# The router's chain of the first pair of batches, emitted in front of the last product of the combined weights

## The chip, the cores and the metric

The kernel runs on one core of one Trainium2 chip. The metric is the device time of one execution in microseconds (us), and of several runs the median. The core has five engines that run side by side, each with its own queue, executed in order: TensorE (PE; its weight loads are listed as PEld), VectorE (DVE), ScalarE (ACT), GpSimd (POOL) and SyncE (SP), which here only starts transfers.

## What is computed

Two layers are added to x (32 batches of 128 tokens with 1024 channels, float32). The first is a mixture of 64 experts. The second maps each token through a dense matrix W plus a low-rank adapter of its batch, and on the result computes a base projection plus a routed low-rank term:

```python
def _L1_cond_ref(x, W, A, Bm, scalings, adapter_idx):
    H = jnp.einsum('btd,od->bto', x, W)
    xa = jnp.einsum('btd,brd->btr', x, A[adapter_idx])
    delta = jnp.einsum('btr,bor->bto', xa, Bm[adapter_idx])
    return H + delta * scalings[adapter_idx][:, None, None]

def _L1_ffn_ref(x, base_w, base_b, router_w, router_b, lora_A, lora_B):
    result = jnp.einsum('bsd,od->bso', x, base_w) + base_b
    logits = jnp.einsum('bsd,ed->bse', x, router_w) + router_b
    probs = jax.nn.softmax(logits.astype(jnp.float32), axis=-1)
    top_vals, top_idx = jax.lax.top_k(probs, 2)
    top_vals = top_vals / jnp.sum(top_vals, axis=-1, keepdims=True)
    gate = jnp.zeros((n, e), x.dtype).at[jnp.arange(n)[:, None], flat_idx].set(flat_val)
    mid = jnp.einsum('nd,edr->ner', xf, lora_A) * gate[:, :, None]
    lora_out = jnp.einsum('ner,erd->nd', mid, lora_B)
    return result + SCALING * lora_out.reshape(b, s, d_out)

x = x + _L0_ffn_ref(_L0_cond_ref(x, ...), ...)
x = x + _L1_ffn_ref(_L1_cond_ref(x, ...), ...)
```

## The kernel before

The first some 2045 us are the mixture of experts. The change lies in the passage from there to the second layer, which takes the rest of the time.

The second layer is done with combined weights: the products of W (and, as a ninth row block, of the adapters' matrices Bm) with the base projection, the low-rank matrices A and the router. They were computed earlier for two of three blocks of columns. The third block is computed in the passage, in `pair_of_rows` (line 1212), four pairs of row blocks with seven products each, and by `multiplied` (line 1259) for the ninth row block. The latter is called the last product here: eight matmuls 128x384 into the bank pcw. Line 1260 copies it with ScalarE into row 9 (`HC + 1`) of `BM`, the big matrix of the second layer, whose rows 0 to 7 belong to the channels, row 8 (`HC`) to the routed low-rank term and row 9 to the adapter.

The tokens are taken in pairs of batches, `q` from 0 to 15. For each pair `X` holds 256 tokens, transposed, in ten chunks: 0 to 7 are channels, chunk 8 is the routed term (mid) and chunk 9 the adapter's (xm). Pair 0 is prepared in the passage, pair q + 1 during iteration q of the loop. The preparation of a pair is this:

- `turned_x1`: two transposes on VectorE from `xq`, the rows loaded from memory, into chunks 0 to 7.
- `inner`: products px on TensorE, which give the low-rank values, the router's logits and the adapter's values; copies into pxs, and xm on VectorE.
- `turned_in` with chunk 9: two transposes on TensorE into a bank pt, a copy on ScalarE into `X`.
- `corrected`: two matmuls pg on TensorE, the adapter's share of the logits.
- `routed` (line 1108): the router's chain. VectorE adds pg to pxs, forms the logits lg and their negated maximum nmaxc; ScalarE computes two exponentials exc; VectorE finds the two largest (topc, idxc), the weights and at last mid. Of its operations only the two exponentials are on ScalarE, none is on TensorE.
- `turned_in` with chunk 8: the transposes pt of mid on TensorE, the copy into `X` on ScalarE.
- `token_sums2`: sums of parts of `X` on VectorE (names ss, and one in place in `X`).

`map_sums` (line 1006) forms on VectorE the four sums of parts of `BM` (names ts1, ts2, ts4, and one in place in `BM`). The loop then has seven products of five matmuls each for every pair, `product2(k)` (bank name pr_c), of which `product2(1)` and `product2(6)` come first: number 1 reads even rows of `BM` and even chunks of `X`, chunk 8 as its last; number 6 reads ts2 and ss2. The px of the next pair follow.

All engines are addressed through `InOrder`, a helper that keeps each engine's instructions in the order in which they are emitted in the source, so that the order of the source's lines is the order in each engine's queue. As this helper issues every operation, the profile shows one line, L219, for nearly all; the names of the tiles tell them apart. The table that ScalarE needs for the exponentials is loaded by an instruction of its own, which the build puts right in front of the first exponential that needs it.

Of the kernel before, what the change touches and what calls it, by code (L numbers as in the profile page):

```python
# [51 lines left out]
def kernel(  # L52
# [147 lines left out]
    def multiplied(n, d, hw, left, pool, tag, pe):  # L200
        w = BLOCKS[n][1] - BLOCKS[n][0]
        pcw = pool.tile([P, 512], F32, name=f"pcw_{n}_{d}", tag=tag)[:, 0:w]
        for j in range(HC):
            if j == HC // 2:
                yield
            pe.matmul(pcw, left[d][:, j, :], hw[:, j, :], start=(j == 0), stop=(j == HC - 1))
        yield pcw
# [859 lines left out]
    def inner(q, X):  # L1067
        px = pc_x.tile([P, 2, NA], F32, name=f"px_{q}", tag="px")
        for t in range(2):
            for j in range(HC):  # L1070
                pe.matmul(
                    px[:, t, :],
                    X[:, j, t * P : (t + 1) * P],
                    pxw[t][:, j, :],
                    start=(j == 0),
                    stop=(j == HC - 1),
                )
        pxs = c2.tile([P, 2, NX], F32, name=f"pxs_{q}", tag="pxs")
        act.copy(pxs, px[:, :, 0:NX])

        xm = c2.tile([P, 2, E2, R], F32, name=f"xm_{q}", tag="xm")
        dve.tensor_tensor(
            xm,
            px[:, :, NX:NA].unsqueeze(2).to_broadcast([P, 2, E2, R]),
            smask[:, 2 * q : 2 * q + 2, :].unsqueeze(3).to_broadcast([P, 2, E2, R]),
            ALU.mult,
        )
        return pxs, xm

    def turned_in(q, X, chunk, m):  # L1090
        pt = pc_t.tile([P, 2, P], F32, name=f"pt_{q}_{chunk}", tag="pt")
        for t in range(2):
            pe.transpose(pt[:, t, :], m[:, t].rearrange("p e r -> p (e r)"), ident)
        act.copy(X[:, chunk, :], pt.rearrange("p t c -> p (t c)"))

    def corrected(q, X, pxs):
        pg = pc_x.tile([P, 2, NX], F32, name=f"pg_{q}", tag="pg")
        for t in range(2):
            pe.matmul(
                pg[:, t, :],  # L1100
                X[:, HC + 1, t * P : (t + 1) * P],
                G_sb[:, 0:NX],
                start=True,
                stop=True,
            )
        return pg

    def routed(q, pxs, pg):
        dve.tensor_tensor(pxs, pxs, pg, ALU.add)

        lg = c2.tile([P, 2, E2], F32, name=f"lg_{q}", tag="lg")
        dve.tensor_tensor(
            lg, pxs[:, :, E2 * R : NX], rb_bc.unsqueeze(1).to_broadcast([P, 2, E2]), ALU.add
        )
        nmax = c2.tile([P, 2], F32, name=f"nmaxc_{q}", tag="nmaxc")
        dve.tensor_reduce(nmax, lg, AX.X, ALU.max, negate=True)
        ex = c2.tile([P, 2, E2], F32, name=f"exc_{q}", tag="exc")
        top = c2.tile([P, 2, 8], F32, name=f"topc_{q}", tag="topc")
        idx = c2.tile([P, 2, 8], U32, name=f"idxc_{q}", tag="idxc")
        for t in range(2):  # L1120
            act.activation(ex[:, t, :], lg[:, t, :], AF.Exp, bias=nmax[:, t : t + 1])
        for t in range(2):
            dve.max(top[:, t, :], ex[:, t, :])
            dve.max_index(idx[:, t, :], top[:, t, :], ex[:, t, :])
        idxf = c2.tile([P, 2, 2], F32, name=f"idxfc_{q}", tag="idxfc")
        dve.tensor_copy(idxf, idx[:, :, 0:2])
        tsum = c2.tile([P, 2], F32, name=f"tsumc_{q}", tag="tsumc")
        dve.tensor_reduce(tsum, top[:, :, 0:2], AX.X, ALU.add)
        rtop = c2.tile([P, 2], F32, name=f"rtopc_{q}", tag="rtopc")
        dve.reciprocal(rtop, tsum)  # L1130
        gv = c2.tile([P, 2, 2], F32, name=f"gv_{q}", tag="gv")
        dve.scalar_tensor_tensor(
            gv,
            top[:, :, 0:2],
            LORA_SCALING,
            rtop.unsqueeze(2).to_broadcast([P, 2, 2]),
            ALU.mult,
            ALU.mult,
        )
        pick = c2.tile([P, 2, 2, E2], F32, name=f"pick_{q}", tag="pick")  # L1140
        for t in range(2):
            dve.tensor_tensor(
                pick[:, t],
                iota_t[:, 0:E2].unsqueeze(1).to_broadcast([P, 2, E2]),
                idxf[:, t, :].unsqueeze(2).to_broadcast([P, 2, E2]),
                ALU.is_equal,
            )
        dve.tensor_tensor(
            pick, pick, gv.unsqueeze(3).to_broadcast([P, 2, 2, E2]), ALU.mult
        )  # L1150
        gate = c2.tile([P, 2, E2], F32, name=f"gate_{q}", tag="gate")
        dve.tensor_tensor(gate, pick[:, :, 0, :], pick[:, :, 1, :], ALU.add)
        mid = c2.tile([P, 2, E2, R], F32, name=f"mid_{q}", tag="mid")
        dve.tensor_tensor(
            mid,
            pxs[:, :, 0 : E2 * R].rearrange("p t (e r) -> p t e r", e=E2),
            gate.unsqueeze(3).to_broadcast([P, 2, E2, R]),
            ALU.mult,
        )
        return mid  # L1160
# [66 lines left out]
    for c in range(HC // 2):  # L1227
        pair = pair_of_rows(c, rows)
        next(pair)
        if c == 3:  # L1230
# [3 lines left out]
            pxs, xm = inner(0, X)  # L1234
# [21 lines left out]
        for _ in pair:  # L1256
            pass
    pg = corrected(0, X, pxs)
    _, pcw = multiplied(2, HC, hw, lefts, pc_p, "pp", pe)
    act.copy(BM[:, HC + 1, :, first:512], pcw.rearrange("p (n c) -> p n c", n=2))  # L1260
    mid = routed(0, pxs, pg)
    turned_in(0, X, HC, mid)
    sums = map_sums(first, 512)
    next(sums)
# [15 lines left out]
    for q in range(NQP):  # L1280
# [31 lines left out]
        if more:  # L1312
            own_columns(ab)
            pxs, xm = inner(q + 1, X)
# [10 lines left out]
        if more:  # L1325
            mid = routed(q + 1, pxs, corrected(q + 1, X, pxs))
# [94 lines left out]
```

## Time and profile before

| | us |
|---|---|
| median of 3 runs | 2678.86 (2677.95 to 2679.11) |
| profiled execution | 2666.59 |
| its span, first to last instruction | 2664.7 |
| TensorE busy | 2642.8 (99%) |
| VectorE busy | 1866.7 (70%) |
| ScalarE busy | 548.5 (21%) |
| mean granted TensorE clock | 0.999 of full |

A matmul in float32 stands in the trace as two records, so the eight matmuls of pcw are shown as x16. Times of instructions are counted from the start of the span. The durations of neighbouring instructions on one engine can overlap a little, since they are pipelined; starts are the safer measure. "ACT_TABLE_LOAD" occurs three times in the whole execution, each of 1.28 us: at the start, when the experts' stage begins (254.40 us), and in the passage.

### The profile page before, as it was taken

The numbers are of one execution on the slowest core, as the hardware profiler recorded it, in microseconds if no ns is written. First come the engines' busy times: TensorE is split into PE (matmuls) and PEld (weight loads), VectorE is DVE, ScalarE is ACT, GpSimd is POOL, SyncE is SP. The second block draws the span as 40 slices with busy tenths as digits, with TensorE's granted clock in tenths as the row PEclk, the third lists the DMA queues.
The fourth block names the chain that finished last, engine by engine and source line by source line (L and its number), as shares of the span: only waits on it lengthen the run. The fifth ranks groups of instructions, "written<-read, shape, count | busy, mean of one in ns | idle before, by whom it ended". The sixth has DMA issues, their size and how long they took to land.

```text
span 2664.7 us, 25525 instructions
## 1 busy us (share of the span) xinstructions
PE 2642.8 (99%) x8942; PEld 1507.4 (57%) x8942; DVE 1866.7 (70%) x3051; ACT 548.5 (21%) x1174; POOL 1051.1 (39%) x854
## 2 busy tenths in 40 slices
PE   8999999999999999999999999999999999999999
PEld 8985555555555555555555555555556655554554
DVE  4456888888888888888888888878776644444442
ACT  2331222222222222222222222222222100000000
POOL 3115546546455464555555555464441100000000
PEclk9999999999999999999999999999999999999999
DMA  9869788788787887887887887878877422222110
GB/s 349 322 242 365 228 253 263 236 251 266 234 258 252 246 269 229 262 259 236 263 249 247 252 255 243 258 251 240 252 230 217 89 67 67 68 67 67 56 38 37
DMA packets 126656, 568.45 MB, mean 213 GB/s; under 512 B 22960, under 2 KB 48816, under 8 KB 100672
## 3 DMA queue, kind: packets, MB, share of 16 engines
q1 hardware_dynamic: 65952, 383.16, 41.0%
q0 software_dynamic: 52384, 161.60, 24.3%
q10 hardware_dynamic: 8192, 22.06, 2.2%
q8 instruction: 72, 1.18, 0.2%
q14 instruction: 56, 0.46, 0.1%
HBM read 459.68 MB, written 123.83 MB: 219 GB/s over the span
## 4 chain that ended last, share of the span: by engine, by line
PE 95%; DMA 3%; POOL 1%; DVE 0%; issue 0%; ACT 0%; ACTq 0%; SPq 0%
PE px L219 27%; PE pr_c L219 18%; PE pv L219 12%; PE py L219 6%; PE pth L219 2%; PE ph L219 2%; PE plog L219 1%; PE pcw L219 1%; DMA hw<-in_head_w 1%; PE pcx L219 1%; PE pmx L219 1%; DMA xin<-hbuf,slot_row 1%; DMA hbuf<-hq 1%; POOL xin L382 1%; PE prk L219 1%
## 5 line engine op out<-in xcount | busy, mean ns | idle before, releaser
L382 POOL DMA_INDIRECT xin<-hbuf,slot_row x512 | 609.5, 1190 | 169.4 <-issue 148.4
L960 POOL DMA_INDIRECT ybuf<-o,slot_tok x128 | 208.5, 1629 | 682.9 <-DVE o L219 234.3
L219 PE MATMUL pr_c<-BM,X 128*128 128x512 f32 x480 | 214.9, 595 | 0.0
L219 POOL DMA_INDIRECT ab<-in_AT,adapter_rows x32 | 37.2, 1163 | 424.4 <-ACT pxw L219 419.0
L306 POOL DMA_INDIRECT rkg<-ranks,row x128 | 157.1, 1227 | 85.1 <-DVE past L219 46.4
L219 PE MATMUL px<-wg,xT 128*128 128x384 f32 x512 | 186.1, 486 | 0.6 <-ACT G_sb L219 0.6
L219 PE MATMUL pv<-t,s 128*128 128x384 f32 x512 | 175.7, 486 | 0.0
L219 PE MATMUL px<-wu,xT 128*128 128x384 f32 x512 | 175.6, 486 | 0.0
L219 PE MATMUL pv<-wu,s 128*128 128x384 f32 x512 | 175.6, 486 | 0.0
L219 PE MATMUL px<-t,xT 128*128 128x384 f32 x512 | 175.6, 486 | 0.0
L219 PE MATMUL py<-wg,xT 128*128 128x384 f32 x512 | 175.6, 486 | 0.0
L219 PE MATMUL px<-t,s 128*128 128x384 f32 x512 | 175.6, 486 | 0.0
L219 DVE TENSOR_TENSOR t<-wu,wg 128x1536 f32<-128x1536 f32 x64 | 113.1, 1768 | 74.4 <-PE pv L219 74.4
L219 DVE STREAM_TRANSPOSE xT<-xin 128x1024 f32<-128x1024 f32 x128 | 151.7, 1220 | 13.2 <-DMA xin<-hbuf,slot_row 10.8
L219 ACT COPY u<-px 128x384 f32<-128x384 f32 x128 | 61.3, 479 | 434.0 <-PE px L219 434.0
L219 PEld LDWEIGHTS pr_c<-BM,X 128*128 128x128 f32 x480 | 89.4, 191 | 100.8 <-issue 100.8
L219 PEld LDWEIGHTS pv<-t,s 128*128 128x128 f32 x512 | 97.2, 190 | 81.0 <-issue 25.8
L219 PE MATMUL pr_c<-ts,ss 128*128 128x512 f32 x320 | 142.4, 592 | 0.0
L219 PEld LDWEIGHTS px<-t,s 128*128 128x128 f32 x512 | 97.3, 190 | 67.8
L219 PEld LDWEIGHTS py<-wg,xT 128*128 128x128 f32 x512 | 97.3, 190 | 67.8
L219 PEld LDWEIGHTS px<-wu,xT 128*128 128x128 f32 x512 | 97.3, 190 | 67.8
L219 PEld LDWEIGHTS pv<-wu,s 128*128 128x128 f32 x512 | 97.3, 190 | 67.8
(1576 smaller groups left out, 4549.6 us busy)
## 6 DMA issues: line engine op xcount, KB each, us to landing
wd<-in_wd SPq DMA_DIRECT2D x64, 1536.0 KB, 8.2
wg<-in_wg SPq DMA_DIRECT2D x63, 1536.0 KB, 8.2
wu<-in_wu SPq DMA_DIRECT2D x63, 1536.0 KB, 10.2
hbuf<-hq ACTq DMA_DIRECT2D x32, 512.0 KB, 8.5
ybuf<-in_x SPq DMA_DIRECT2D x32, 512.0 KB, 8.5
xq<-ybuf SPq DMA_DIRECT2D x64, 256.0 KB, 5.0
out_y<-out_c SPq DMA_DIRECT2D x31, 512.0 KB, 2.7
x<-in_x_q SPq DMA_DIRECT2D x28, 512.0 KB, 7.7
```

The source lines that it names most:

```text
L219: return lambda *args, **kw: kept(op(*args, **kw))
L306: nc.gpsimd.indirect_dma_start(out=some["rk"][:, s, :, :].rearrange("p i t -> p (i t)"), out_offset=None, in_=ranks.rearrange("e b i t -> ...
L382: nc.gpsimd.indirect_dma_start(out=xin[:, q, :], out_offset=None, in_=quarters, in_offset=bass.IndirectOffsetOnAxis(ap=slot_row[:, s : s + ...
L960: nc.gpsimd.indirect_dma_start(out=ybuf, out_offset=bass.IndirectOffsetOnAxis(ap=slot_tok[:, s : s + 1], axis=0), in_=o[j], in_offset=None ...
```

## The change

One line moves. The router's chain of pair 0 is emitted after `corrected` and ahead of the last product and its copy, instead of after them:

```diff
     pg = corrected(0, X, pxs)
+    mid = routed(0, pxs, pg)
     _, pcw = multiplied(2, HC, hw, lefts, pc_p, "pp", pe)
     act.copy(BM[:, HC + 1, :, first:512], pcw.rearrange("p (n c) -> p n c", n=2))
-    mid = routed(0, pxs, pg)
     turned_in(0, X, HC, mid)
     sums = map_sums(first, 512)
     next(sums)
```

The loop's own calls of `routed` are not touched.

## The prediction

> **What bounds the kernel now.** I read the shares of busy time first, then the chain that ended last, then the waits of TensorE, and only then the stretch of the change.
>
> ```profile
> PE 2642.8 (99%) x8942; PEld 1507.4 (57%) x8942; DVE 1866.7 (70%) x3051; ACT 548.5 (21%) x1174; POOL 1051.1 (39%) x854
> PE 95%; DMA 3%; POOL 1%; DVE 0%; issue 0%; ACT 0%; ACTq 0%; SPq 0%
> ```
>
> TensorE is busy for 99% of the span and is 95% of the chain, so a change pays only where TensorE stands still or runs below its full clock. The view of waits, for TensorE alone, has few entries:
>
> ```profile
> PE ph L219 <- DMA w<-in_cond_w,cond_rows: 9.0, 1, 9.0
> PE pt L219 <- DVE mid L219: 4.7, 1, 4.7
> PE pth L219 <- DVE h L219: 1.8, 1, 1.8
> ```
>
> The second is the place of the change: once, for 4.7 us, the transposes of mid wait for VectorE. The same view from 2115 us to the end is empty, so whatever is won here reaches the end whole. The timelines of TensorE, ScalarE and VectorE show how the wait comes about (start, duration, engine, operation; in brackets the idle time before it):
>
> ```profile
> 2093.09 5.32 PE L219 MATMUL pcw<-hw,WB_b 128*128 128x384 f32 x16
> 2103.13 0.69 PE L219 MATMUL pt<-ident,mid 128*128 128x128 f32 x2 [4.72 <-DVE mid L219]
> 2103.61 5.68 PE L219 MATMUL pr_c<-BM,X 128*128 128x512 f32 x10
> 2109.13 4.45 PE L219 MATMUL pr_c<-ts,ss 128*128 128x512 f32 x10
> 2113.42 4.30 PE L219 MATMUL px<-pxw,X 128*128 128x152 f32 x32
> ```
>
> ```profile
> 2092.88 0.32 ACT L219 COPY ts<-pmx 128x192 f32<-128x192 f32 x1 [2.28 <-PE pmx L219]
> 2098.45 0.48 ACT L219 COPY BM<-pcw 128x384 f32<-128x384 f32 x1 [5.25 <-PE pcw L219]
> 2098.94 1.28 ACT L219 ACT_TABLE_LOAD   x1
> 2100.24 0.49 ACT L219 ACTIVATE exc<-lg,nmaxc 128x8 f32<-128x8 f32 x2
> 2103.86 0.37 ACT L219 COPY X<-pt 128x256 f32<-128x256 f32 x1 [3.13 <-PE pt L219]
> ```
>
> ```profile
> 2094.44 0.17 DVE L219 TENSOR_REDUCE nmaxc<-lg 128x2 f32<-128x16 f32 x1
> 2100.57 0.17 DVE L219 MAX8 topc<-exc 128x8 f32<-128x8 f32 x1 [5.96 <-ACT exc L219]
> ...
> 2104.26 0.83 DVE L219 TENSOR_TENSOR ss<-X 128x640 f32<-128x640 f32 x1
> ...
> 2111.15 2.36 DVE L219 STREAM_TRANSPOSE X<-xq 128x1024 f32<-128x1024 f32 x2
> ```
>
> The router's maximum is ready at 2094.61, but its exponentials stand on ScalarE behind the copy of the last product, which TensorE ends at 2098.42. The table load and the exponentials come after that copy, and VectorE's remaining router steps after those. The wait costs more than its length, as the stretches of 3.41 us behind it show (the number after the POOL column is the granted TensorE clock):
>
> ```profile
> 2099.25:2102.66 3.41, 0.00 (x0) 0.00 (x0) 1.81 (x15) 1.47 (x3) 0.00 (x0) 1.00 0.18 32
> 2102.66:2106.07 3.41, 2.94 (x5) 1.50 (x6) 3.26 (x5) 0.77 (x3) 1.01 (x1) 0.50 0.00 0
> 2106.07:2109.50 3.43, 3.43 (x9) 1.52 (x8) 3.43 (x5) 0.00 (x0) 1.62 (x1) 1.00 0.12 38
> ```
>
> An idle stretch is followed by one of equal length at clock 0.50, in which the first product of the loop runs.
>
> **The change, part by part.** It adds and removes no instruction and no transfer. TensorE's order stays (pg, pcw, pt, pr_c), as routed puts nothing on TensorE; so does VectorE's, as the last product and its copy put nothing there; SP and POOL are not touched. On ScalarE the two exponentials, with the table load that stands ahead of them, move in front of the copy of pcw into BM.
>
> Step 1, the router's chain. The copy that precedes them on ScalarE ends at 2092.88 + 0.32 = 2093.20. The load then takes 1.28, to 2094.48; its cover is the last product, on TensorE until 2098.42. The maximum is there at 2094.61. Where the loop runs the same chain with the table in place, VectorE's MAX8 starts 0.37 us after the maximum; so here it starts at 2094.98. From MAX8 to the end of mid takes 2100.57 to 2103.08 = 2.51 us. Mid is ready at 2097.49.
>
> Step 2, TensorE. The records of pcw start 5.17/16 = 0.32 us apart, the last at 2097.92, so the transposes may start at 2098.25. Mid is there 0.76 us before: the wait of 4.72 us goes, and with it the slow clock. At full clock a pair of transposes takes 0.22 us start to start (those of xm at 2089.80 to 2090.02) and a product of five matmuls 4.29 (2109.13 to 2113.42), against 0.48 and 5.52 here. So on TensorE alone: transposes 2098.25, first product 2098.47, second 2102.76, px 2107.05, which is 6.37 us ahead of 2113.42 (4.88 of start, 0.26 and 1.23 of clock).
>
> The rule of the Trainium skill that speaks against this is in "ScalarE: Activation LUTs", section "What ACT_TABLE_LOAD costs": a switch of the table set is a load of about 1283 ns and a drain of about 1380 ns more. The load agrees (1.28 us); of a drain the row shows nothing, since the load starts 0.01 us after the copy and the exponential 0.02 us after the load. By the rule mid would come at 2097.49 + 1.38 = 2098.87, the transposes 0.62 us after TensorE is free, and the gain of the sum below would be 5.4 us instead of 5.9. I go by the row.
>
> Step 3, the copy that is now behind. It starts at 2098.45 as before if the exponentials are done, which they are from about 2095.2. The copy of the transposes into X (chunk 8) follows it. It needs the transposes (start + 0.42, as at 2089.80 to 2090.22: 2098.67) and ScalarE, whose copies overlap their neighbour by 0.1 us (the next one starts at 2104.13, before 2103.86 + 0.37): 2098.45 + 0.48 - 0.1 = about 2098.82.
>
> Step 4, what is late next. VectorE's sum ss started 0.40 us after that copy's start (2103.86 to 2104.26), so it starts at 2099.22, 5.04 us earlier. Behind it VectorE is unbroken to the transposes of the second pair of batches: they shift by 5.04 too. The first ended at 2111.15 + 1.23 = 2112.38, hence 2107.34, and px waits for it: TensorE would be there at 2107.05. The handoff is 0.05 (mid at 2103.08 to pt at 2103.13), and the weight load of px, hidden before, is, I estimate, exposed for 0.1 to 0.2 us (it takes 0.19). So px starts at about 2107.5 and the gain is 5.9 us. Bounds: 6.4, TensorE alone, and 5.7, if the copies on ScalarE don't overlap at all.
>
> Other work in the stretch hides: the sum ts1 needs nothing of pcw (it reads even rows of BM; the copy writes row 9) and runs while VectorE waits for X; ts2 ends at 2107.02 - 5.04 = 2101.98, 0.8 us before the second product can start. The bias and the rows of the second pair land by about 2100 (the DMA share is 0.86 from 2092 to 2100 and 0.10 in the next 1 us), and VectorE wants them only from 2105.5 on. The copies into pxw follow the copy into X on ScalarE, and POOL's two gathers follow these; both shift with it and are wanted an iteration later.
>
> The sum: 5.9 us of the profiled execution's 2666.59 (span 2664.7 and 1.9 around it). The median of the timed runs, 2678.86, lies 12.3 us higher; nothing in the stretch scales with that, so I take the gain as absolute: 2678.86 - 5.9 = 2673.0.
>
> **Rivals.**
> - *The timed executions of before did not pay the slow clock.* For: the idle 4.72 us is only 1.3 us longer than one of the 3.41 us stretches, so where the stretches lie may decide, and the three runs lie 1.16 us apart. Against: the profiled one did pay it. With a full clock, px of before would be ready at 2103.13 + 0.22 + 8.58 = 2111.93 and wait for VectorE's 2112.38; only the shift of VectorE is won, 5.0 us: 2673.9. That the clock is judged in free-running windows of about 3.4 us, so that the phase varies by run, is what the Trainium skill says in "TensorE: Matmul & The Clock Gate", section "What's actually happening"; the trace agrees in one place, with a drop 4.24 us after TensorE stopped.
> - *The router's chain ends after pcw.* A load of twice its row, 2.57 us, puts mid at 2098.77, leaves 0.52 us of idle in front of the transposes and puts the copy into X at 2099.19 and ss at 2099.59: a shift of 4.67, gain 5.5, 2673.4. Against: no row shows more than 1.28.
> - *VectorE or a transfer holds px longer,* by 1 to 3 us: gain 3 to 5, about 2674.9. For: VectorE is without a break there and 70% busy overall. Against: all that it reads has landed by 2100.
> - *Slower: ScalarE's head is blocked.* The table load waits, in the built instruction stream, for a count of a DMA queue. If that count were reached only with the rows of the second pair, at about 2100, load and exponentials would start 1.06 us later than the 2098.94 of now, and the copy of pcw and then the product of ts would be held behind them: 2679.9. It decides from 2098.94 on. Against: the count is 240, and the waits for that queue a few instructions on are for 672, so it is an early transfer.
> - *The order on ScalarE doesn't change:* 2678.9. Against: the built stream shows the exponentials in front of the copy.
>
> **How the numbers follow.** Forecast 0.60, full clock before 0.20, late chain 0.07, VectorE or transfer 0.06, blocked head 0.03, no change 0.04. The predicted time is the forecast's. The range runs from 2678.86 - 6.4 less 0.9 (the distance of the fastest run from the median) = 2671.6 to the time of the clock rival and the same distance above, with a little of the third rival: 2675.0. A difference of 0.2%, 5.4 us, is about what a measurement of this kernel tells from no change, and it lies between the forecast's 5.9 and the clock rival's 5.0. Faster by more: the forecast and half of the late chain, 0.64. Within: the rest, 0.34. Slower by more: 0.02, a blocked head that lasts beyond 2104.3.
>
> **What would show it.** In the profile of the changed kernel: table load at about 2093.2 (counted as here), MAX8 at 2095.0, mid done before pcw ends, no wait of pt, clock 1.00 throughout, first product in 4.3 us, px at about 2107.5 with 0.2 to 0.5 us of waiting for X. A load that starts after 2098, a wait of pt for mid, or a wait of px beyond 1 us would make the prediction wrong.

## The result and the profile after

The kernel with the change takes 2671.17 us (median of 19 runs, 2662.76 to 2679.95), the kernel before 2678.86 (19 runs, 2666.37 to 2687.87). The ratio is 0.9974, with a 95% interval of 0.9964 to 0.9985: 7.0 us less, 4.0 to 9.6 by the interval. The two medians lie 7.7 us apart.

The profiled executions alone would mislead. That of the change took 2673.24 us, longer than the 2666.59 of before. The loss lies ahead of the change, where both kernels have the same instructions in the same order. TensorE's waits of the kernel after (engine and name, what it waited for, us in total, times, longest):

```profile
PE ph L219 <- DMA w<-in_cond_w,cond_rows: 9.0, 1, 9.0
PE px L219 <- ACT u L219: 5.2, 1, 5.2
...
PE px L219 <- DVE X L219: 0.3, 1, 0.3
```

The second line is a wait of 5.2 us at 266 us of the span, at the start of the experts' stage, which the first profile of before doesn't have; other profiles of both kernels have it with 10.4 (before) and 10.8 us (after). The clock differs too: from 174.30 to 184.70 us it is 0.51 here and 1.00 there. So pcw starts at 2105.57 here and at 2093.09 there, and executions of one and the same kernel differ by some 20 us (2666.37 to 2687.87 for before). What the change does is therefore read as distances from the first record of pcw. The entry "pt waits for mid: 4.7" of before is gone; the last line is new.

TensorE's timeline of the kernel after, then ScalarE's, then VectorE's:

```profile
2105.57 5.32 PE L219 MATMUL pcw<-hw,WB_b 128*128 128x384 f32 x16
2110.72 0.38 PE L219 MATMUL pt<-ident,mid 128*128 128x128 f32 x2
2110.94 4.46 PE L219 MATMUL pr_c<-BM,X 128*128 128x512 f32 x10
2115.24 4.45 PE L219 MATMUL pr_c<-ts,ss 128*128 128x512 f32 x10
2119.97 4.37 PE L219 MATMUL px<-pxw,X 128*128 128x152 f32 x32 [0.28 <-DVE X L219]
```

```profile
2105.36 0.32 ACT L219 COPY ts<-pmx 128x192 f32<-128x192 f32 x1 [2.28 <-PE pmx L219]
2105.69 1.28 ACT L219 ACT_TABLE_LOAD   x1
2107.12 0.49 ACT L219 ACTIVATE exc<-lg,nmaxc 128x8 f32<-128x8 f32 x2
2110.93 0.48 ACT L219 COPY BM<-pcw 128x384 f32<-128x384 f32 x1 [3.31 <-PE pcw L219]
2111.30 0.38 ACT L219 COPY X<-pt 128x256 f32<-128x256 f32 x1
```

```profile
2109.54 0.42 DVE L219 TENSOR_TENSOR mid<-pxs,gate 128x256 f32<-128x256 f32 x1
...
2111.71 0.83 DVE L219 TENSOR_TENSOR ss<-X 128x640 f32<-128x640 f32 x1 [0.68 <-ACT X L219]
...
2118.59 2.36 DVE L219 STREAM_TRANSPOSE X<-xq 128x1024 f32<-128x1024 f32 x2
```

The load and the exponentials run under pcw, mid is ready at 2109.96 while pcw lasts until about 2110.7, the transposes follow pcw without a gap. From the first pcw to the first px of the second pair, a distance called D from here on, it takes 2119.97 - 2105.57 = 14.40 us; before it was 2113.42 - 2093.09 = 20.33. The difference, 5.93 us, reaches the end: from pcw to the last product of the loop it is 557.84 us (2663.41 - 2105.57) against 563.70 (2656.79 - 2093.09), 5.86 less.

The clock, in stretches of pcw, the first and the second product of the kernel after (from:to, length, then busy us of PE, PEld, DVE, ACT and POOL with counts, the granted clock, the share and GB/s of the DMA engines):

```profile
2105.50:2110.70 5.20, 5.20 (x18) 3.06 (x18) 4.28 (x20) 1.95 (x4) 0.00 (x0) 1.00 0.95 230
2110.70:2115.20 4.50, 4.50 (x13) 2.12 (x12) 3.79 (x6) 1.15 (x4) 2.55 (x2) 1.00 0.45 83
```

In these stretches TensorE never stops and the clock stays at 1.00, where before it fell to 0.50.

### The profile page after: what moved, and what is told of

The parts are those of the page before. It is cut to its first block, busy times and chain, and to the rows that moved or that the text cites. A ratio compares the mean times of both kernels' runs of the same rounds, so it can differ in the third digit from the quotient of the medians.

```text
span 2671.4 us, 25525 instructions
## 1 busy us (share of the span) xinstructions
PE 2647.9 (99%) x8942; PEld 1510.8 (57%) x8942; DVE 1866.8 (70%) x3051; ACT 548.5 (21%) x1174; POOL 1054.1 (39%) x854
## 4 chain that ended last, share of the span: by engine, by line
PE 96%; DMA 2%; DVE 1%; another core or an unknown queue 1%; SPq 0%; ACT 0%; issue 0%; DVEq 0%; ACTq 0%
PE px L219 27%; PE pr_c L219 18%; PE pv L219 12%; PE py L219 6%; PE pcw L219 2%; PE ph L219 2%; PE plog L219 2%; PE pth L219 2%; PE pcx L219 1%; PE pmx L219 1%; PE prk L219 1%; DMA WB_b<-in_WB 1%; DMA hbuf<-hq 1%; PE pcv L219 0%; PE pmv L219 0%
## 5 line engine op out<-in xcount | busy, mean ns | idle before, releaser
L219 PEld LDWEIGHTS px<-t,xT 128*128 128x128 f32 x512 | 98.0, 192 | 74.3 <-ACT u L219 5.8
```

The source lines that it names most:

```text
L219: return lambda *args, **kw: kept(op(*args, **kw))
```

## The experiments

**The two kernels again.** The first question was whether D is a property of the kernel or of one execution. Kernel before, unchanged:

> The kernel before, profiled a second time. Measure D: from the first record of pcw to the first record of px of the second pair on TensorE, 20.33 us in the first profile of before and 14.40 in that of the change. Theory (the passage is fixed by the order on ScalarE; what differs between executions lies in other stages): the wait of pt for mid is 4.7 us again, D is 19.4 to 20.4, wherever pcw starts in the span. If the slow clock of 3.4 us depends on where the execution happens to lie, D is 19.5 with the clock at 1.00 in the first product, or 20.3 with it at 0.50 for 3.4 us. Rival (the passage itself varies by some us like the whole time does): D differs from 20.3 by 2 us or more.

Kernel of the change, unchanged:

> The change, profiled a second time. Theory: D is 14.3 to 14.4 again and the clock 1.00 from pcw to px, while the start of pcw in the span moves by some us with the stages ahead. Rival (the gain is a matter of how one execution fell): D differs by over 1 us.

The change again gave D = 14.40 us, at clock 1.00, with pcw starting 5.6 us later in the span. Before again had the wait of pt at 4.72 us, but D was 2119.89 - 2098.61 = 21.28, over the expected 19.4 to 20.4. Its clock, in stretches:

```profile
2103.90:2106.65 2.75, 0.04 (x1) 0.00 (x0) 0.48 (x5) 2.25 (x4) 0.00 (x0) 1.00 0.56 94
2106.65:2109.10 2.45, 0.44 (x2) 0.45 (x3) 2.25 (x12) 0.00 (x0) 0.00 (x0) 0.50 0.00 0
2109.10:2113.25 4.15, 4.15 (x7) 1.71 (x6) 4.00 (x6) 0.77 (x3) 2.53 (x2) 0.50 0.06 16
2113.25:2115.60 2.35, 2.35 (x7) 0.99 (x6) 2.35 (x4) 0.00 (x0) 0.10 (x1) 0.95 0.09 28
```

The clock fell 2.7 us after TensorE had stopped and stayed at 0.50 for 6.8 us, 4.35 of which lie on the first product (the 0.95 of the last line is some 0.24 us more at 0.50); in the first profile of before it was 3.4 us, of which about 2.9 were work. Two more profiles of before were taken to see what may happen there:

> The kernel before, profiled a third time. D (first pcw to first px of the second pair) was 20.33 with the clock at 0.50 for one stretch of 3.4 us, and 21.28 with two such stretches; without one it would be the 19.24 of the kernel whose gap was filled. Theory (the router's wait is fixed, and only the number of slow stretches behind it differs between executions): the wait of pt is 4.72 us, and D is one of 19.2, 20.3 to 20.4 and 21.2 to 21.3, by none, one or two stretches. Rival (something else in the passage varies): D off these by over 0.2 us.

> The kernel before, profiled a fourth time, as the third: wait of pt 4.72 us; D one of 19.2, 20.3 to 20.4 and 21.2 to 21.3, by the number of slow stretches. If the phase of the stretches is chance, not all four profiles of before show the same number.

The third had D = 2126.12 - 2104.39 = 21.73, the fourth 2127.56 - 2107.20 = 20.36. The wait was 4.73 and 4.72 us. So the number of slow stretches (two and one) is not the whole of it: in the third they begin 1.1 us before pt, in the second profile 2.0 us before, and it is the slow time lying on work that counts. Its first product:

```profile
2114.45 0.69 PE L219 MATMUL pt<-ident,mid 128*128 128x128 f32 x2 [4.73 <-DVE mid L219]
2114.93 7.06 PE L219 MATMUL pr_c<-BM,X 128*128 128x512 f32 x10
2121.82 4.46 PE L219 MATMUL pr_c<-ts,ss 128*128 128x512 f32 x10
```

From product to product it takes 6.89 us instead of 4.29. The expectation, D one of three values, missed for the third profile; that the wait is fixed and only the slow clock behind it varies held in all four. None of the four escaped the slow clock.

**The gap filled.** What is the wait worth without the slow clock? The filler's result is used by nothing:

```diff
     mid = routed(0, pxs, pg)
+    filler = pc_p.tile([P, 512], F32, name="filler", tag="pp")[:, 0 : 2 * half]
+    for j in range(7):
+        pe.matmul(filler, lefts[HC][:, j, :], hw[:, j, :], start=(j == 0), stop=(j == 6))
     turned_in(0, X, HC, mid)
```

> Order of before, plus seven matmuls 128x384 into a spare bank behind pcw, some 4.5 us, so that TensorE does not stand still while mid is late; their result is not used. Theory (of the 5.9 us, 5.0 are the shift of VectorE's work and only 0.9 the slow clock): the clock stays at 1.00, the first product takes 4.3 us, mid is as late as before, px waits about 0.5 us for the transposes of the second pair; D is 19.4 to 19.6, a gain of 0.8 to 0.9. Rival (the slow clock costs its whole 1.5 us on the path): D is 18.9 or less. Rival (the slow clock does not come from standing still): clock 0.50 in the first product again, D 20.3.

TensorE's timeline of this kernel:

```profile
2096.62 5.32 PE L219 MATMUL pcw<-hw,WB_b 128*128 128x384 f32 x16
2101.78 4.68 PE L219 MATMUL filler<-hw,WB_b 128*128 128x384 f32 x14
2106.67 0.44 PE L219 MATMUL pt<-ident,mid 128*128 128x128 f32 x2 [0.21 <-DVE mid L219]
2106.94 4.46 PE L219 MATMUL pr_c<-BM,X 128*128 128x512 f32 x10
...
2115.86 2.82 PE L219 MATMUL px<-pxw,X 128*128 128x152 f32 x20 [0.16 <-DVE X L219]
```

(The listing ends at 2118.5 us, so it counts only the first 20 of the 32 records of px.) The clock stays at 1.00, mid is as late as before (pt 10.05 us after pcw against 10.04), and px waits for VectorE. D is 2115.86 - 2096.62 = 19.24, 1.09 below the first profile of before; expected were 19.4 to 19.6. The copy into X now starts 0.47 us after pt, not 0.73, since the transposes run at full clock, and that moves VectorE's chain too. So of the 5.93 us between the two first profiles 4.84 are the shift of mid and what follows on VectorE, and 1.09 the slow clock; in the other profiles of before the clock costs 2.04, 2.49 and 1.12.

**The gap filled in part.** The same with `range(3)`, to see how short a wait still lets the clock fall:

> Order of before with three filling matmuls behind pcw in place of seven (1.9 us), so that TensorE stands still for about 2.8 us, less than one stretch of 3.4 us; their result is not used. Theory (the clock falls when a stretch of 3.4 us passes with TensorE nearly all of it idle; a wait of 3.30 us, 2.9 of it within one stretch, was enough): with 2.8 us the clock stays at 1.00 and D is 19.2 to 19.3. Rival (a shorter wait is enough too): clock 0.50 for one or two stretches, D 20.0 to 21.3.

```profile
2113.50:2116.30 2.80, 0.05 (x1) 0.00 (x0) 2.25 (x16) 0.43 (x2) 0.00 (x0) 1.00 0.00 1
2116.30:2119.75 3.45, 3.42 (x6) 1.83 (x7) 3.30 (x4) 0.77 (x3) 1.35 (x2) 0.51 0.00 0
```

After 2.79 us of idle the clock fell all the same, and D was 2126.88 - 2106.29 = 20.59. The theory that nearly a whole stretch of 3.4 us must be idle is refuted; how much is enough is taken up in the last section.

**The table load alone.** Is it the exponentials' place or the load that matters?

```diff
+    early_exp = c2.tile([P, 1], F32, name="early_exp", tag="early_exp")
+    act.activation(early_exp, ones[:, 0:1], AF.Exp)
     _, pcw = multiplied(2, HC, hw, lefts, pc_p, "pp", pe)
```

> Order of before, plus one exponential of a 128x1 constant on ScalarE in front of the copy of pcw, so that the table load comes early and the router's two exponentials stay behind the copy. Theory (the exponentials' place behind the copy is the cause, and the load is only 1.3 us of it): the router's exponentials start right behind the copy, 1.3 us earlier than before against pcw; the wait of pt falls from 4.7 to 3.4 us; D (first pcw to first px of the second pair, 20.33 before, 14.40 with the change) is 18.0 to 19.2, by the clock that follows. Rival (the table load is what costs): D comes near the change's, 14.4 to 15.5.

ScalarE's timeline of this kernel:

```profile
2115.01 1.28 ACT L219 ACT_TABLE_LOAD   x1
2116.31 0.20 ACT L219 ACTIVATE early_exp<-ones 128x1 f32<-128x1 f32 x1
2120.24 0.48 ACT L219 COPY BM<-pcw 128x384 f32<-128x384 f32 x1 [3.74 <-PE pcw L219]
2120.62 0.49 ACT L219 ACTIVATE exc<-lg,nmaxc 128x8 f32<-128x8 f32 x2
```

The load is hidden, but the exponentials still queue behind the copy, though their maximum has long been there. The wait of pt falls to 3.30 us, D to 2134.07 - 2114.88 = 19.19, as the theory had it, with one slow stretch of the clock behind the wait. The early load takes 1.42 us off the wait of 4.72; the other 3.30 are the place behind the copy.

**The copy on another engine.** The line of before with `dve.tensor_copy` in place of `act.copy`:

> Order of before, with the copy of pcw on VectorE instead of ScalarE. It then stands ahead of the router's first sums on VectorE. Theory (the chain is late as long as any of its steps queues behind that copy, on whichever engine): the chain starts when pcw ends, the table load is hidden, mid is only about 0.4 us earlier than before, the wait of pt is 4 to 4.6 us, D is 18.9 to 20.0. Rival (ScalarE with its load has to be freed, that is enough): exponentials early, wait of pt under 1 us, D about 14.4.

VectorE's timeline of this kernel:

```profile
2104.70 0.56 DVE L219 COPY BM<-pcw 128x384 f32<-128x384 f32 x1 [4.60 <-PE pcw L219]
2105.17 0.43 DVE L219 TENSOR_TENSOR pxs<-pxs,pg 128x272 f32<-128x272 f32 x1
...
2106.37 0.17 DVE L219 MAX8 topc<-exc 128x8 f32<-128x8 f32 x1 [0.37 <-ACT exc L219]
```

ScalarE is free, its load is done under pcw (2099.46 to 2100.74, pcw starts at 2099.33), and still almost nothing is won: now the router's first sum queues behind the copy on VectorE. The wait of pt is 4.28 us (expected 4 to 4.6). D, at 20.97, is over the expected 20.0, by two slow stretches as in two profiles of before; it is the rival, 14.4, that falls.

**What is late after the change.** The new wait of px, 0.28 us, was traced in two ways. First the copy of pcw behind the copy into X:

```diff
     mid = routed(0, pxs, pg)
     _, pcw = multiplied(2, HC, hw, lefts, pc_p, "pp", pe)
-    act.copy(BM[:, HC + 1, :, first:512], pcw.rearrange("p (n c) -> p n c", n=2))
     turned_in(0, X, HC, mid)
+    act.copy(BM[:, HC + 1, :, first:512], pcw.rearrange("p (n c) -> p n c", n=2))
```

> The change, with the copy of pcw into BM moved further back, behind the copy of mid's transposes into X. Theory (with the change, VectorE's chain from X is what px of the second pair waits for, and the copy of pcw holds X up by about 0.15 us): the copy into X starts 0.1 to 0.2 us earlier against pcw, px waits 0.1 to 0.2 us instead of 0.28, D (first pcw to first px of the second pair, 14.40 with the change) is 14.2 to 14.3; the sum ts2, which needs the copy of pcw, stays hidden. Rival (ts2 becomes the wait): the second product waits for ts2, D is 14.4 or more.

The copy into X starts 5.58 us after pcw instead of 5.73, and D is 2120.07 - 2105.82 = 14.25, both as expected. Second, the bias out of the way of VectorE's transposes:

```diff
-    dve.tensor_tensor(bias[:, 1, :], bias[:, 1, :], bias[:, 0, :], ALU.subtract)
...
             X = turned_x1(q + 1, xq, side)
+        if q == 0:
+            dve.tensor_tensor(bias[:, 1, :], bias[:, 1, :], bias[:, 0, :], ALU.subtract)
```

> The change, with the subtraction of the two halves of the bias (0.68 us on VectorE) moved behind the transposes of the second pair, which px waits for. Theory (only VectorE's place in line still holds px): the transposes start 0.6 us earlier against pcw, px does not wait, D is 13.95 to 14.0, TensorE's own time (14.40 with the change). Rival (px waits for a transfer or for ScalarE's copies): D stays 14.3 to 14.4. In the timed runs the ratio to before is 0.9974 as for the change, or at most 0.0002 lower, which lies within the interval.

```profile
2105.97 5.32 PE L219 MATMUL pcw<-hw,WB_b 128*128 128x384 f32 x16
...
2115.64 4.45 PE L219 MATMUL pr_c<-ts,ss 128*128 128x512 f32 x10
2119.94 4.30 PE L219 MATMUL px<-pxw,X 128*128 128x152 f32 x32
```

D is 13.97 and px has no wait: this is TensorE's own time for the passage. Its ratio to the kernel before is 0.9969 (0.9958 to 0.998), median 2671.26 us of 10 runs; that is 0.0005 below the ratio of the change, where at most 0.0002 was expected, and well within the interval. By the trace it is 0.43 us better than the change; the timed runs can't tell the two apart.

## Why the prediction was right, point by point

- *Step 1, the chain under pcw.* Right. Counted from the first pcw, the load was forecast at 0.11 us and came at 0.12, MAX8 at 1.89 and came at 1.89, mid at 4.40 and came at 4.39. No second price of the table load appeared: the exponentials start at 1.55, after the maximum, as forecast from the loop's own chain. The 1.38 us of drain that the Trainium skill states beside the load ("ScalarE: Activation LUTs", section "What ACT_TABLE_LOAD costs") show in no run here: in the kernel with the early load the small exponential starts 0.02 us after the load. The forecast's two sums for a dearer load (with the drain, and the rival of the late chain) put all of the extra time on mid, though the load was to end at 2094.48, 0.13 us before the maximum; so each makes mid late by about 0.1 us too much.
- *Step 2, TensorE.* Right: transposes at 5.16 forecast and 5.15 measured, first product 5.38 and 5.37, second 9.67 and 9.67.
- *Step 3, the copy behind.* Right: the copy into X was forecast at 5.73 and came at 5.73, held up 0.15 us by the copy of pcw, as the run with that copy moved back shows.
- *Step 4, what is late next.* Right: VectorE's sums and transposes moved by 5.04 us against pcw (transposes at 13.02 after pcw, 18.06 before), and px waits for them, from 14.41 by the forecast and 14.40 measured. The kernel with the bias moved shows that VectorE's place in line is the whole of that wait.
- *The sum.* 5.9 us for the profiled execution, against 5.93. The time forecast, 2673.0, is 1.8 above the median, and the ratio's 7.0 us are 1.1 above the forecast. By the four profiles, the term that is too small for the mean is the slow clock: in the first profile of before it costs 1.09 us of D, in the four 1.09 to 2.49. Their mean D is (20.33 + 21.28 + 21.73 + 20.36) / 4 = 20.93, which is 6.5 us above the change's. What remains to 7.0 is well inside the interval. The forecast's price of the slow clock, 0.9 us (5.9 less the 5.0 of the rival without it), fits the first and the fourth profile and is too little for the other two.
- *The range* was narrower than the timed runs can support. It is 3.4 us wide and rests on three runs of before that lay 1.16 us apart; 19 runs spread over 21.5 us, and the interval on the difference is 5.6 us wide. That 2678.86 x 0.9974 = 2671.9 falls into it is in part luck, and the median, 2671.17, lies 0.4 us below its lower end. What bears the forecast out is D and the starts in the traces.
- *The rival of the full clock* fell: in the four profiles the slow clock is always paid, and costs more than was forecast, not less. It had let the timed executions of before escape the slow clock since 4.72 us is only little longer than one stretch. The runs show that 2.79 us of idle are enough. A wait of 4.72 us puts at least half of itself, 2.36 us, into one stretch of 3.41, and by the last section less than that was enough; in four profiles it never escaped and was followed by one or two slow stretches. That without the slow clock little more than VectorE's shift remains was right: 4.84 us by the filled gap, 5.0 by the rival.
- *VectorE or a transfer holding px by 1 to 3 us* did not occur: px waits 0.28 us, for VectorE.
- *The late chain, the blocked head and an unchanged order* are excluded by ScalarE's timeline above: the load starts 0.01 us after the copy ahead of it and takes 1.28, and the exponentials stand in front of the copy of pcw.

## What to carry to other kernels

An engine that is busy for a fifth of the time can still decide the end, by the order of its queue: look, at each long wait of the bounding engine, for what stands ahead of the awaited work in its queue, and whether that needs something later than the awaited work does. A copy that must wait for a long product belongs behind short steps whose inputs are there, whichever engine takes it; and a wait of TensorE of some 3 us costs more than its length. Where executions differ by more than the change is worth, measure in the trace from an instruction just ahead of the change to one behind it.

## What the runs showed of the hardware that was not expected

The clock of TensorE fell to 0.50 after waits of 2.79, 3.30, 4.28 and 4.7 us, and stayed there for one stretch of 3.41 us or for two (6.83). After a wait of 1.78 us (pth, at 264.57 us in the first profile of before) it stayed at 1.00. The length of a wait does not decide alone. Within a run the slow stretches begin whole multiples of 3.4133 us apart (in the third profile of before at 256.49 and 2113.34, 544 times that), and it matters how a wait lies against them. The experts' stage of that profile shows it, in such stretches:

```profile
253.08:256.49 3.41, 1.52 (x6) 0.92 (x6) 0.00 (x0) 0.48 (x1) 2.50 (x4) 1.00 0.69 240
256.49:259.90 3.41, 3.41 (x7) 1.90 (x6) 0.00 (x0) 0.00 (x0) 2.52 (x3) 0.50 0.37 117
259.90:263.31 3.41, 2.26 (x7) 0.97 (x6) 0.00 (x0) 0.00 (x0) 0.95 (x1) 1.00 0.25 77
263.31:266.73 3.42, 2.47 (x8) 1.44 (x8) 1.81 (x4) 2.28 (x3) 0.00 (x0) 1.00 0.64 198
```

A wait of 1.89 us lies whole in the first stretch, and the second runs at 0.50. A longer one, of 2.10 us (262.16 to 264.26), is split over the last two, and the clock stays at 1.00, as it does after a split wait of 2.13 us at 272.27. In the kernel after, 1.86 us whole in one stretch (274.85 to 276.70) left the clock at 1.00. So, by these few waits, some 1.9 us of idle within one stretch were enough. A second slow stretch followed where TensorE still stood still for 1.1 to 2.0 us at the start of the first one, and none where that was 0.5 us or less. This is not the whole rule: between 168 and 179 us the clock fell in every profile but the first of before, around a wait of only 0.74 us among a router's short products (plog), and why is open.

The Trainium skill, in "TensorE: Matmul & The Clock Gate", section "HAM oscillation — how this bites in real kernels", gives as the rule that TensorE should have no idle gaps above about 3.4 us; here shorter ones were enough, and the measurement decides.

Why the experts' stage starts with a wait of 4 to 11 us in some executions of either kernel and not in others is open; it lies ahead of the change, and no experiment here bears on it.
